# One core, two transformer layers: transposes between the scores, a key buffer filled by POOL, and a split normalization in layer 1's attention

## The chip, the core and the metric

The kernel runs on one core of a Trainium2 chip. A core has five engines that run their own instruction streams in order and wait for each other through semaphores: PE (TensorE, matrix multiplication), DVE (VectorE), ACT (ScalarE), POOL (GpSimd) and SP (SyncE), which here only issues DMA transfers. The metric is the device time of one execution in microseconds (us); lower is better. "Weight load" (PEld) is PE's loading of the stationary operand.

## The reference

The input `x` is [8, 512, 256] in float32. Two pre-norm layers follow each other, each `x = x + attention(layernorm(x))`, then `x = x + ffn(layernorm(x))`:

- layer 0: causal attention, 16 heads of 16; then a gated FFN whose inputs and weights are quantized to FP4 in blocks of 16;
- layer 1: attention with biases in which a query sees only the 64 keys up to itself; then a gated FFN with integer weights.

The part that the change touches is layer 1's attention:

```python
q = (x @ Wq + bq).reshape(B, S, H, hd).transpose(0, 2, 1, 3)   # k, v likewise
scores = jnp.einsum('bhqd,bhkd->bhqk', q, k) * scale
allowed = (j <= i) & (i - j < WINDOW)                           # WINDOW = 64
attn = jax.nn.softmax(jnp.where(allowed, scores, NEG_INF), axis=-1)
out = jnp.einsum('bhqk,bhkd->bhqd', attn, v)
return out.transpose(0, 2, 1, 3).reshape(B, S, D) @ Wo + bo
```

## The kernel before

**Stages.** The whole `x` stays in SBUF, a tile `x{b}` for each of the 8 batch elements ("batches" below). The four parts of the reference run one after another; from the spans of their instructions in the trace they take about 0 to 540 us (attention 0), 540 to 797 us (FFN 0), 797 to 1120 us (attention 1) and 1120 to 1287 us (FFN 1). One function, `attention`, writes both attentions; `banded` is true for layer 1.

**Units and quads.** A unit is (batch, m): 8 of the 16 heads of a batch. A quad is half of a unit, four heads; `quads[i]` with i = 4 c + r is the r-th quad of batch c. `body` first does some opening work and then loops over i. Quad i's pass does, in this order: the scores of quad i+2 in query order (`scores`, tiles `s`), from which DVE takes the row maxima (tiles `mx`, L540); the scores of quad i in key order (`Outputs.band`, tiles `t`), with the maxima multiplied in as twelve extra rows; ACT's exponential of them (tiles `ex`, L655); POOL's selects that zero what the mask forbids (L128); and for the quads before it the products with the values (`banded_sums`, tiles `po`), the copy `oT`, and the normalized output.

**Where q and k come from.** For a unit, `pieces` projects the transposed, normalized input: matmuls into `pq` or `pk` (through `project`, L303), ACT's biased copy into bfloat16 (`qp`/`kp` part 0, L420), and DVE's remainder (`qr`/`kr`, L421). `store` then makes two more bfloat16 parts of the remainder: ACT copies part 1 (L431), POOL subtracts to get part 2 (L434), and SP sends the three parts to HBM (L437). `land` fetches them back in six slots per head, `qq` by four transfers and `kk` by three (L447), in a layout in which one 96-row product gives the six products of parts that matter. There are three `qq`/`kk` buffers; two are made by `QK` (`qq_both`, `kk_both`), the third (`qq2`, `kk2`) belongs to the attention's own pool and is made when `body` starts. Rows 96 and up of every `kk` are constants ("ones", L353) that meet the maxima.

For batches 1 to 7 of layer 1 both the weights and the input are split in a high and a low float32r half; `project` then does three pairs of halves, two matmuls (one for each 128 of the 256 inputs) a pair. The high half of the transposed input is `yT1` (ACT, L191), its low half lies in `room` (DVE, L192).

**The order of instructions** comes from a planner: it orders each engine's instructions by its own estimate of when they are ready, save those marked by `pin` (`keep_in_program_order`), which stay in the order in which they were written. PE's matmuls of the attention are pinned, ACT's copy of part 1 (L431) is pinned, ACT's normalization (`normalize`, L168) and exponentials are not. PSUM tiles come from two rings: three two-bank tiles (`s`, `t`) and two one-bank tiles (`pm`, `pt_c`, `pq`, `pk`, `pv`, `po` and others take turns), so a matmul into a new tile waits for the readers of the one two tiles back.

**Opening of layer 1's body.** FFN 0's last projections end, the third key buffer gets its ones (DVE), POOL clears the padded value buffers, `norm(1)` normalizes batch 1 on ACT (`by`), then come the scores of quad 1, the maxima of quad 0 as rows (`pm`, L567, with an ACT copy L574 and a DVE copy L575), the two transposes of batch 1 (`turned`: `pt_c`, L185, whose readers are ACT L191 and DVE L192), and the projections, stores and fetches of unit (1, 0). The biases' rows (`bo_rows`, `bo_halves`, `two_rows`) are made meanwhile by POOL memsets and ACT copies (L1109 to L1121).

**Normalization of later batches.** In quad 1 of batch c, batch c+2 is normalized: four ACT instructions, two in each half of the pass.

Of the kernel before, what the change touches and what calls it, by code (L numbers as in the profile page):

```python
# [19 lines left out]
P = 128  # L20
B, S, D = 8, 512, 256
# [25 lines left out]
def tile_two_layers(  # L47
# [246 lines left out]
        nc.scalar.copy(full, src)  # L294
        nc.gpsimd.tensor_tensor(lo, full, hi.bitcast(F32), ALU.subtract)

    def project(dst, lhs, rhs):

        n = 0
        pairs = PAIRS if len(lhs) == 2 else ((0, 0),)  # L300
        for l, r in pairs:
            for e in range(NE):
                pin(nc.tensor.matmul(  # L303
                    dst, lhsT=lhs[l][:, e, :], rhs=rhs[r][:, e, :],
                    start=(n == 0), stop=(n == NE * len(pairs) - 1),
                ))
                n += 1
# [38 lines left out]

        return t.bitcast(BF16).rearrange("p t a (h two) -> p t a h two", two=2)[:, :, :, :, 1]

    def units_tiles(pool, n, what):
        q = pool.tile([P, 8, S], BF16, tag=f"qq{n}", name=f"qq{n}_{what}", bufs=1)  # L350
        k = pool.tile([P, 8, S], BF16, tag=f"kk{n}", name=f"kk{n}_{what}", bufs=1)

        nc.vector.tensor_copy(  # L353
            k[KF:].bitcast(F32), own[KF:].unsqueeze(2).to_broadcast([32, 8, S // 2])
        )
        return q, k
# [3 lines left out]
    def attention(home, banded, stats, norm, spin, wq_s, wk_s, wv_s, qcol, kcol, bv_bc, post, filler):  # L360
# [40 lines left out]
        def pieces(b, m, w, col, name):  # L401

            pp = psum1(f"p{name}_{b}_{m}")
            ws = halved("qk".index(name), b, w)
            project(pp, [x[:, :, m * P : (m + 1) * P] for x in ws], xT[b])
            if home[2]:
                t = home[0].tile(
                    [P, 3, S], BF16, tag=f"{name}p", name=f"{name}p_{b}_{m}", bufs=home[2]
                )
            else:  # L410
                t = home[3](f"{name}p_{b}_{m}")
            r = home[0].tile(
                [P, S], F32, tag="rem" if home[2] else "full", name=f"{name}r_{b}_{m}",
                bufs=home[2] or 1,
            )
            if col is None:
                nc.scalar.copy(t[:, 0], pp)
                nc.vector.tensor_tensor(r, pp, t[:, 0], ALU.subtract)  # L418
            else:
                nc.scalar.activation(t[:, 0], pp, AF.Identity, bias=col[:, m : m + 1])  # L420
                nc.vector.scalar_tensor_tensor(  # L421
                    r, pp, col[:, m : m + 1], t[:, 0], ALU.add, ALU.subtract
                )
            return t, r
# [44 lines left out]
        def turned(b, c):  # L469
            if c == 0:  # L470
                fine = banded and b
                xT[b] = [home[0].tile(
                    [P, NE, S], F32R if fine else F32, tag="yT1", name=f"yT{int(banded)}_{b}",
                    bufs=home[1],
                )]
                if fine:
                    xT[b].append(FINE["x"])
            spin(b, c, xT[b])
# [72 lines left out]
        def maxima(i):  # L551


            mx = MX[i]
            for a in range(2):
                nc.vector.tensor_tensor(
                    mx[:, :, a + 1, :], mx[:, :, a, :], upper(mx)[:, :, a, :], ALU.subtract
                )
# [184 lines left out]

        def body():

            q, k = units_tiles(home[0], 2, int(banded))
            QQ.append(q)
            KK.append(k)
            padded_values(home[0], 1, nc.gpsimd)
            if banded:  # L750
                for n in range(2):
                    v = home[0].tile([P, NT, H, HP], F32, tag=f"vq{n}", name=f"vq{n}", bufs=1)
                    nc.gpsimd.memset(v[WIN:, 0], 0.0)
                    VQ.append(v)
                shifted(0)
                fine = fine_halves(home[0])
                next(fine)
            norm(1)
            for i in range(1 if banded else 0, 2):
                for s in scores(i):  # L760
                    s()
                maxima(i)
            max_rows(0)
            for c in range(NE):
                turned(1, c)
            load_q(units[2])
            stores(units[2], 0)
            load_k(units[2])
            stores(units[2], 1)
            land(units[2])  # L770


            last = trail = None
            ending = filler(home[0]) if banded else None
            for i in range(len(quads) + (2 if banded else 1)):
                ts, ss, cur = [], [], None
                if i < len(quads):
                    cur = Outputs(i)
                    ts = cur.tiles()
                    if i + 2 < len(quads):  # L780
                        ss = scores(i + 2)
                c, r = i // 4, i % 4
                nT = 2 if banded else 6
                side = {p: [] for p in range(nT)}

                def at(p, fn):
                    side[p].append(fn)

                p1, p2, p3 = (1, 0, 0) if banded else (1, 2, 3)
                f1, f2, f3 = (0, 1, 1) if banded else (0, nT - 2, nT - 1)  # L790
                if banded and i + 1 < len(quads):
                    at(p3, lambda: max_rows(i + 1))

                if last is not None:
                    at(p1, lambda: last.banded_sums() if banded else last.sums((2, 3)))
                    at(p1, lambda: last.copy())
                done = trail if banded else last
                if done is not None and not banded:
                    at(p2, lambda: done.finish())

                if r == 0 and c + 1 < B:
                    at(f2 if banded else f1, lambda: values(c + 1, 0))
                if r == (2 if banded else 0) and c + 1 < B:
                    at(f1 if banded else f2, lambda: values(c + 1, 2))
                if r == 2 and c + 2 < B:
                    at(f3 if banded else f1, lambda: turned(c + 2, 0))
                    at(f3, lambda: turned(c + 2, 1))
                if r == 0 and c + 2 < B:
                    at(f3, lambda: stats(c + 2))
                if r == 1 and c + 2 < B and not banded:  # L810
                    for t in range(NT):
                        at(t, lambda t=t: norm(c + 2, [t]))
                if banded and r == 3 and c + 1 < B:
                    at(f1, lambda: shifted(c + 1))
                if r % 2 and i // 2 + 3 < len(units):
                    at(f1, lambda: load_q(units[i // 2 + 3]))
                    at(f2, lambda: load_k(units[i // 2 + 3]))
                    at(f3, lambda: stores(units[i // 2 + 3], 0))
                for p, fn in tail.pop(i, ()) if banded else ():
                    at(p, fn)  # L820
                if done is not None and banded:
                    at(p2, lambda: done.finish())
                if i + 1 < len(quads) and not banded:
                    at(p3, lambda: max_rows(i + 1))
                if cur and not banded:
                    at(f3, lambda: cur.sums((0, 1)))
                if r == 1 and c + 2 < B and banded:
                    for t in range(NT):
                        at(t // 2, lambda t=t: norm(c + 2, [t]))
                if r % 2 == 0 and i and i // 2 + 2 < len(units):  # L830
                    at(f1 if banded else p1, lambda: stores(units[i // 2 + 2], 1))
                    at(f1 if banded else f2, lambda: land(units[i // 2 + 2]))
                for p in range(max(len(ts), nT if last or done else 0)):
                    if p < len(ss):
                        ss[p]()
                        step()
                    if p < len(ts):
                        ts[p]()
                        step()
                    for fn in side[p]:  # L840
                        fn()
                    if banded and p:
                        next(fine, None)
                    if banded and i > 4 * B - 6:
                        next(ending, None)
                if ss:
                    maxima(i + 2)
                last, trail = cur, last
            for _ in ending or ():
                pass  # L850
            for n in sorted(tail) if banded else ():
                for p, fn in tail.pop(n):
                    fn()
# [615 lines left out]
```

## Time and profile before

| what | value |
|---|---|
| time, median of 3 runs | 1280.49 us (1279.89 to 1282.59) |
| the profiled execution's own time | 1288.33 us, span 1286.5 us from first to last instruction |
| mean granted PE clock | 0.954 of full speed |
| attention 1, 797 to 1120 us: busy PE, DVE, POOL, ACT | 277.4, 229.6, 211.4, 172.2 of 323 us |
| the same stretch: mean granted PE clock, DMA share | 0.95, 0.61 |

The profiled execution took 7.8 us longer than the median of the runs. A row of the page's groups, or of an answer on waits, gives a sum over instructions with one source line; a row of the timeline gives start, duration, engine, line, operation, tiles, and in brackets how long the engine stood idle before and what ended that. Idle time of an engine that isn't the bottleneck costs nothing. The label of a wait is inferred, and can name the wrong tile where several were waited for. A line "SPq" is the time at SP's queue of issuing a transfer, its own wait included.

### The profile page before, as it was taken

What the parts mean: (1) busy time and instruction counts of PE and PEld (TensorE: products, weight loads), DVE (VectorE), ACT (ScalarE), POOL (GpSimd) and SP (SyncE); (2) the same over time, 40 slices, a digit from 0 to 9 for tenths busy, and PEclk for the clock granted to TensorE, in tenths of its full rate; (3) what the DMA queues carried; (4) which work ended last, traced back from release to release, by engine and by line L of the source; (5) the groups of instructions that cost most, each with busy time, mean ns of one, the idle gap of its engine ahead of it and who ended that gap; (6) DMA issues with size and microseconds to landing.
All of it is one profiled execution on the core that took longest, in us unless ns stands there. A gap on an engine that the chain in (4) does not pass through costs nothing. (4 is left out here: it accounts for less than half of the span.)

```text
span 1286.5 us, 27214 instructions
## 1 busy us (share of the span) xinstructions
PE 1100.3 (86%) x10910; PEld 819.8 (64%) x10910; DVE 943.5 (73%) x1603; ACT 659.7 (51%) x1008; POOL 698.8 (54%) x821
## 2 busy tenths in 40 slices
PE   4778989788998888788888887788998898889998
PEld 2444444444554445787888777567777776668887
DVE  4699896698788885789799857677776686545553
ACT  3255656465674676444444333455555554455553
POOL 5165564465445566655555533576766675534443
PEclk9899999898998999899999988899999998999999
DMA  8644334443453311000000025476675676000001
GB/s 229 140 96 87 86 74 86 79 94 67 91 116 74 81 18 50 1 1 1 1 1 1 1 72 105 100 165 155 144 149 125 141 164 163 2 1 33 33 26 43
DMA packets 51634, 99.53 MB, mean 77 GB/s; under 512 B 6702, under 2 KB 43568, under 8 KB 44848
## 3 DMA queue, kind: packets, MB, share of 16 engines
q1 hardware_dynamic: 50624, 96.96, 33.9%
q8 instruction: 88, 1.44, 0.5%
q10 hardware_dynamic: 816, 0.79, 0.2%
q14 instruction: 42, 0.34, 0.1%
q0 software_dynamic: 64, 0.00, 0.0%
HBM read 61.02 MB, written 29.36 MB: 70 GB/s over the span
## 5 line engine op out<-in xcount | busy, mean ns | idle before, releaser
L128 POOL TENSOR_SCALAR_AFFINE_SELECT ex<-ex 64x512 f32<-64x512 f32 (+2 forms) x448 | 268.9, 603 | 226.1 <-ACT ex L620 131.3
L620 ACT ACTIVATE ex<-t 128x1024 f32<-128x1024 f32 (+1 forms) x192 | 167.9, 882 | 125.3 <-PE t L609 114.1
L517 DVE TENSOR_REDUCE mx<-s 128x2 f32<-128x1024 f32 (+2 forms) x192 | 196.7, 1036 | 41.1 <-PE s L506 40.3
L1319 POOL TENSOR_TENSOR hT<-gh,hT 128x512 fp32r<-128x512 f32 x48 | 61.6, 1290 | 89.6 <-ACT hT L1318 66.1
L655 ACT ACTIVATE ex<-t 128x1024 f32<-128x1024 f32 x64 | 65.5, 1023 | 86.6 <-PE t L647 81.9
L501 PE MATMUL s<-kk_both,qq_both 96*128 96x512 bf16 (+3 forms) x352 | 84.6, 323 | 20.8 <-DVE mx L517 10.9
L506 PE MATMUL s<-cmask,minus_b 128*128 128x128 bf16 (+2 forms) x352 | 90.4, 257 | 0.0
L540 DVE TENSOR_REDUCE mx<-s 128x8 f32<-128x1024 f32 x64 | 77.6, 1215 | 15.3 <-PE s L535 15.2
L282 POOL TENSOR_TENSOR h<-h,sc_h 128x704 f32<-128x704 f32 x32 | 45.1, 1410 | 79.4 <-DVE h L281 73.6
L674 PE MATMUL po<-ex,vp 128*32 128x512 f32 (+3 forms) x1024 | 83.4, 442 | 1.3 <-DVE kr L418 1.3
L609 PE MATMUL t<-qq_both,kk_both 108*128 108x512 bf16 (+3 forms) x352 | 70.9, 306 | 9.1 <-ACT ex L620 4.7
L1386 DVE SCALAR_TENSOR_TENSOR gh<-ggu,gsl 128x512 f32<-128x512 f32 x48 | 33.2, 691 | 57.1 <-ACT gsl L1384 56.6
L1260 PE MATMUL pd<-wd_high,hT 128*128 128x256 f32 x384 | 61.7, 299 | 11.6 <-DVE hT L1251 7.0
L277 ACT ACTIVATE mg_h<-h 128x704 bf16<-128x704 f32 x32 | 25.2, 788 | 82.7 <-POOL h L229 82.7
L1227 PE MATMUL gu<-wg_wgh,fyT 128*128 128x352 f32 x224 | 65.3, 333 | 2.4 <-DVE h L1234 2.4
L501 PEld LDWEIGHTS <-qq_both 96*128 96x128 bf16 x352 | 33.0, 103 | 51.6 <-issue 38.0
L229 POOL TENSOR_TENSOR h<-h,rc_h 128x704 f32<-128x704 f32 x32 | 46.4, 1449 | 34.1 <-DVE rc_h L228 18.8
L1260 PEld LDWEIGHTS pd<-wd_high,hT 128*128 128x128 f32 x384 | 53.7, 200 | 16.4 <-DVE hT L1251 10.7
L1227 PE MATMUL gu<-wu_wuh,fyT 128*128 128x352 f32 x224 | 62.7, 322 | 0.0
L1375 PE MATMUL ggu<-yT,wg_r 128*128 128x512 f32 x192 | 57.6, 412 | 2.1 <-DVE yT L1319 1.1
L279 DVE SCALAR_TENSOR_TENSOR h<-mg_h,h 128x704 f32<-128x704 bf16 x32 | 40.6, 1269 | 22.4 <-ACT mg_h L277 22.4
L674 PEld LDWEIGHTS po<-ex,vp 128*32 128x32 f32 x1024 | 27.1, 109 | 43.9 <-issue 29.8
(335 smaller groups left out, 3167.9 us busy)
## 6 DMA issues: line engine op xcount, KB each, us to landing
q_hbm<-qp SPq DMA_DIRECT2D x90, 128.0 KB
k_hbm<-kp SPq DMA_DIRECT2D x90, 128.0 KB
qq_both<-q_hbm SPq DMA_DIRECT2D x44, 256.0 KB
kk_both<-k_hbm SPq DMA_DIRECT2D x22, 384.0 KB
qq_both<-q_hbm SPq DMA_DIRECT2D x44, 128.0 KB
kk_both<-k_hbm SPq DMA_DIRECT2D x22, 256.0 KB
qq<-q_hbm SPq DMA_DIRECT2D x20, 256.0 KB
vq<-vp SPq DMA_DIRECT2D x8, 512.0 KB
```

The costliest lines, as they stand in the source:

```text
L128: nc.gpsimd.affine_select(out=t, in_=t, compare_op=ALU.is_ge, fill=0.0, base=base, pattern=[[0, n] for n in shape[1:-1]] + [[sign, shape[- ...
L501: pin(nc.tensor.matmul(bank[:, a * w : (a + 1) * w], lhsT=q[:KF, hs[j], t * P : w], rhs=k[:KF, hs[j], :w], start=(a == 0), stop=False, ski ...
L506: pin(nc.tensor.matmul(bank.rearrange("p (i k) -> p i k", k=w)[:, :, t * P :], lhsT=minus_b, rhs=cmask[:, : len(part), :], start=False, st ...
L517: nc.vector.tensor_reduce(dst, src, AX.X, ALU.max)
L540: nc.vector.tensor_reduce(mx[:, t2 : t2 + 2, :], sc.rearrange("p t (j k) -> p t j k", k=P), AX.X, ALU.max)
L609: pin(nc.tensor.matmul(bank[:, a * w : (a + 1) * w], lhsT=k[: KF + 12, self.hs[j], t * P : (t + 1) * P], rhs=q[: KF + 12, self.hs[j], t * ...
L620: nc.scalar.activation(ex[:, :banks, :used], sc[:, :banks, :used], AF.Exp, scale=QSCALE)
L655: nc.scalar.activation(ex, sc, AF.Exp, scale=QSCALE)
L674: pin(nc.tensor.matmul(self.o[HP * j : HP * (j + 1), t * P :], lhsT=vp[:, t, 4 * c + j, :], rhs=self.ex[t, j], start=(t == 0), stop=(t == ...
L1227: nc.tensor.matmul(gu[:, i, :352], lhsT=YT[b][l][:, e, t * P : (t + 1) * P], rhs=w[r][:, e, f], start=(n == 0), stop=(n == 3 * NE - 1),)
L1260: nc.tensor.matmul(pd[:, :D], lhsT=hT[l][:, k, :], rhs=wd_halves[r][:, k, :], start=(l == r == k == 0), stop=(l == 1 and k == NH - 1),)
L1319: engine.tensor_tensor(lo, src, hi.bitcast(F32), ALU.subtract)
```

## The change

Four edits, all for layer 1's attention (layer 0 keeps its code paths):

1. `project` gets a flag `last`, used by `pieces`: the three pairs of halves go high-high, low weight with high input, high weight with low input. Before, the low input was in the second pair.
2. The ones of the third key buffer are written by POOL and not by DVE.
3. In the opening, `max_rows(0)` comes first, each of the two transposes of batch 1 stands after one of the two score tiles of quad 1, and `maxima(1)` is written after unit (1, 0)'s fetches.
4. In the program, the normalization of batch c+2 moves from both halves of quad 1's pass to the second half of quad 1 and the first half of quad 2.

```diff
-    def project(dst, lhs, rhs):
+    def project(dst, lhs, rhs, last=False):
...
         for l, r in pairs:
+            if last:
+                l, r = r, l
             for e in range(NE):
...
-    def units_tiles(pool, n, what):
+    def units_tiles(pool, n, what, engine=nc.vector):
...
-        nc.vector.tensor_copy(
+        engine.tensor_copy(
             k[KF:].bitcast(F32), own[KF:].unsqueeze(2).to_broadcast([32, 8, S // 2])
         )
...
-            project(pp, [x[:, :, m * P : (m + 1) * P] for x in ws], xT[b])
+            project(pp, [x[:, :, m * P : (m + 1) * P] for x in ws], xT[b], True)
...
-            q, k = units_tiles(home[0], 2, int(banded))
+            q, k = units_tiles(home[0], 2, int(banded), nc.gpsimd if banded else nc.vector)
...
-            for i in range(1 if banded else 0, 2):
-                for s in scores(i):
+            if banded:
+                max_rows(0)
+                for c, s in enumerate(scores(1)):
                     s()
-                maxima(i)
-            max_rows(0)
-            for c in range(NE):
-                turned(1, c)
+                    turned(1, c)
+            else:
+                for i in range(2):
+                    for s in scores(i):
+                        s()
+                    maxima(i)
+                max_rows(0)
+                for c in range(NE):
+                    turned(1, c)
             load_q(units[2])
             stores(units[2], 0)
             load_k(units[2])
             stores(units[2], 1)
             land(units[2])
+            if banded:
+                maxima(1)
...
-                if r == 1 and c + 2 < B and banded:
-                    for t in range(NT):
-                        at(t // 2, lambda t=t: norm(c + 2, [t]))
+                if r in (1, 2) and c + 2 < B and banded:
+                    for t in (0, 1) if r == 1 else (2, 3):
+                        at(2 - r, lambda t=t: norm(c + 2, [t]))
```

What the planner makes of it, read from the order of the built instructions on each engine: no instruction is added or dropped but for the one copy that goes from DVE to POOL. ACT's four normalizations of each batch stand where they stood. What edit 4 does change is another instruction: for the units (2, 1), (3, 1), (4, 1), (5, 1) and (6, 1), the pinned copy of the key's part 1 (L431) now stands ahead of ACT's exponential of the first half of quad 2, where it stood behind it and behind the copy of the maxima. POOL's subtraction (L434) of these units goes ahead of the four selects of that exponential, and on SP the second and third store of the key parts go ahead of the first two fetches of `qq`. Edits 1 to 3 change nothing beyond the opening but the order of the matmuls within a projection. In the opening, DVE's order becomes: maxima of the first score tile, copy of quad 0's maxima rows, low half of transpose 0, maxima of the second score tile, low half of transpose 1. ACT copies both transposes before it touches the bias rows.

## The prediction

> **What bounds the kernel now.** I read the page first, then the busy time by stage, then who waited for whom in attention 1, then the timelines of the places concerned.
>
> ```profile
> PE 1100.3 (86%) x10910; PEld 819.8 (64%) x10910; DVE 943.5 (73%) x1603; ACT 659.7 (51%) x1008; POOL 698.8 (54%) x821
> ```
>
> PE is busy for 86% of the span, and in attention 1 for 277.4 of 323 us; the next, DVE, for 229.6. So in this stage a gap of PE that goes away is time, and work of the others counts where PE waits for it. PE's waits there, from 797 to 1100 us (total, times, longest):
>
> ```profile
> PE s L535 <- DMA kk_both<-k_hbm: 8.2, 3, 6.0
> PE pk L303 <- ACT oT L695: 4.9, 1, 4.9
> PE pq L303 <- DVE room L192: 3.7, 1, 3.7
> ...
> PE s L535 <- DMA q_hbm<-qp: 2.2, 1, 2.2
> ...
> PE s L535 <- DMA kk<-k_hbm: 1.2, 1, 1.2
> ```
>
> Two kinds matter: one wait of 3.7 us in the opening, and score matmuls (L535) that wait for fetched q and k. The opening, PE, then DVE:
>
> ```profile
> 799.62 1.40 PE L185 MATMUL pt_c<-ident,by 128*128 128x128 f32 x8
> 804.71 1.22 PE L303 MATMUL pq<-yT,qkv_wg 128*128 128x512 f32 x2 [3.68 <-DVE room L192]
> ```
>
> ```profile
> 797.97 2.51 DVE L353 COPY kk<-own 32x2048 f32<-32x2048 f32 x1
> 800.51 2.35 DVE L540 TENSOR_REDUCE mx<-s 128x8 f32<-128x1024 f32 x2
> 802.89 0.95 DVE L575 COPY qq_both<-qq_both 12x1536 bf16<-12x1536 bf16 x1
> ...
> 803.97 0.68 DVE L192 TENSOR_TENSOR room<-pt_c,yT 128x512 fp32r<-128x512 f32 x1
> ```
>
> `pq` needs the PSUM tile of transpose 0, whose last reader is DVE's low half, which ends at 804.65 because three DVE pieces stand before it. Afterwards PE runs slow: the twelve matmuls of `pq` and `pk` take 804.71 to 809.77, 0.42 us each, against 0.24 later on (859.65 to 861.18).
>
> The waits for fetched data come at the first score tile in quad 0 of a batch, the scores of unit (c, 1):
>
> ```profile
> 886.89 0.30 PE L535 MATMUL s<-kk,qq 96*64 96x64 bf16 x6 [2.17 <-DMA q_hbm<-qp]
> ...
> 925.25 0.36 PE L535 MATMUL s<-kk_both,qq_both 96*64 96x64 bf16 x7 [1.17 <-DMA kk_both<-k_hbm]
> ...
> 963.38 0.30 PE L535 MATMUL s<-kk_both,qq_both 96*64 96x64 bf16 x6 [0.71 <-issue]
> ...
> 1004.80 0.36 PE L535 MATMUL s<-kk,qq 96*64 96x64 bf16 x7 [1.21 <-DMA kk<-k_hbm]
> ```
>
> These are the units (2,1) to (5,1); (6,1) at 1046.12 has no gap, and (7,1) waits 6.05 us at 1083.35. ACT and SP before the second of them:
>
> ```profile
> 909.47 1.03 ACT L655 ACTIVATE ex<-t 128x1024 f32<-128x1024 f32 x1 [1.89 <-PE t L647]
> 910.52 0.58 ACT L574 CAST qq<-pm 12x512 bf16<-12x512 f32 x1
> 911.12 0.62 ACT L431 CAST kp<-kr 128x512 bf16<-128x512 f32 x1
> ```
>
> ```profile
> 914.61 0.58 SPq L437 DMA_DIRECT2D k_hbm<-kp  x1
> 915.25 0.91 SPq L447 DMA_DIRECT2D qq_both<-q_hbm  x2
> 917.59 1.23 SPq L447 DMA_DIRECT2D kk_both<-k_hbm  x3
> ```
>
> The key's remainder `kr` is ready at 907.85 (DVE 907.10 + 0.75), but its copy comes at 911.12, POOL's subtraction at 913.42, the last store at 914.61, the last fetch by 918.8.
>
> **What the Trainium skill says.** "TensorE: Matmul & The Clock Gate", section "What's actually happening": PE's clock halves after an idle window of about 3.4 us and comes back after as much activity. The trace agrees: 0.42 against 0.24 us above, and a granted clock of 0.50 from 888 to 890 us, after the 2.17 us gap. "DMA: Bandwidth & Descriptors", section "Issuing engines are not separate DMA queues": all transfers share 16 engines and interleave. The trace fits: the DMA share is 0.94 to 1.08 from 917 to 925 us, so an earlier fetch is worth only what room it finds. "GPSIMD Engine Reference", section "Engine selection": for one input POOL runs at about the line rate. Its 512-element casts of layer 0 (L433) take 0.609 us.
>
> **The change part by part.**
>
> *Ones by POOL, transposes between scores (edits 2 and 3).* After the change DVE's chain is: last `x` addition to 797.94; `pm` goes first on PE (797.4 to 797.8), the first score tile is done by about 798.8; maxima 798.9 to 800.1 (half of 2.35); ACT's rows (L574) still end at 800.31, since the normalizations before them end at 799.64; DVE's copy 800.4 to 801.35; low half 0 to 802.05, as transpose 0 follows the last normalization and ACT copies it by 800.95. `pq` can start at 802.1, 2.6 us earlier. The second maxima (to 803.2) and low half 1 (to 803.9) follow. PE's longest gap there shrinks to about 0.5 us, so I expect the warm 0.24 us a matmul.
>
> *Pair order (edit 1).* With the new order the first four matmuls need only high halves and end at 803.05; the last two wait for low half 1, so `pq` ends at about 804.4. In the old order four would stand behind it: 0.5 us more. From batch 2 on `room` is complete long before: no wait for it shows, so the swap costs and brings nothing there.
>
> So PE would finish `pk` at about 805.8 for 809.8. But ACT has work in between. POOL's memsets of 797.60 to 802.16 come later by the length d of the ones' copy, which no row shows on POOL: 2048 elements at the cast's rate are 4 x 0.609 = 2.4 us; from below 1.8, the memset of 2048 (L327), from above 3.9, twice the 1.94 us of a two-input operation on 1024. `two_rows` (ended 803.28) then ends at 805.7, and ACT's `qp`, next in its queue, starts there in place of 807.67. Behind it are `kp`, the two parts, and the first exponential (813.31); POOL's twelve selects, `rs_c`, the normalizations of batch 2 and PE's second big wait (4.92 us, `pk` at 826.35) hang on those. The gain that reaches them is 2.0 us for ACT's start plus 1.2 for `pk` being ready without ACT's 1.52 us wait ahead of `kp`: 3.2 us. With d at 1.8 or 3.9 it is 3.8 or 1.7; it is nothing from d of 5.6 up.
>
> *Key part moved ahead (edit 4).* In unit (3,1) the copy can go at 907.85 and ends at 908.5, in the 1.89 us in which ACT waits for `t`: that idle time hides it. POOL subtracts from 909.1 (end of the query's part) to 910.3, in its idle time before the select at 910.57. The stores are out by 910.9 and not 915.2; the four `qq` fetches by 912.8, `kk` (2.3 us after the store, as before) by 914.5 for 918.8. The values' shifts (L398, L399), next in SP's queue, move up too, and together these are 768 + 768 + 896 KB, at the 200 GB/s seen from 919 to 927 us 12.2 us, so done by 923.5 with `kk` about 1 us before; PE wants it at 924.1. The gaps then go: 2.17 + 1.17 + 0.71 + 1.21 = 5.3 us. After the first gap PE also ran slow: from 886.89 to the end of the transposes before the values took 7.68 us, in the next batch 7.88 less 1.76 of output matmuls = 6.12; that adds 1.5. I take off 0.4 for unit (6,1), where `kr` ends at 1031.24, after the exponential that started at 1029.92, and which now waits for it; and 0.9 because the margin above is only 1.6 us. Sum: 5.5 us; from below 0 (fetches no sooner), from above 6.8.
>
> Layer 0, FFN 0 and FFN 1 issue the same instructions. What follows attention 1, the 6.05 us wait of unit (7,1) included, has its order unchanged and moves as a whole.
>
> Sum against the profiled execution: 1288.3 - 3.2 - 5.5 = 1279.6. The runs have the median 1280.49; I take the same difference from it: 1271.8, rounded to 1272.
>
> **Rivals.**
>
> *The fetches come no sooner.* The DMA engines are full from 917 on, and the shifts of the values (896 KB) move up with the fetch. If `kk` still lands when all is through, only the opening gains: 1280.5 - 3.2 = 1277.3. Against it: from 905 to 911 the DMA share is 0.04 to 0.35, so there is room before.
>
> *The opening gains nothing.* POOL takes over 5 us for the ones; ACT's `qp` comes as late as before. Then 1280.5 - 5.5 = 1275. Against it: the cast's rate.
>
> *Slower: ACT's exponential behind the key part.* ACT is in order, and the copy now waits for `kr` ahead of the exponential. It decides as soon as `kr` ends later than 0.62 us before `t` is ready. In (6,1) it does, and the exponential slips by 1031.24 + 0.62 - 1029.92 = 1.9 us; POOL's selects and the next maxima rows queue behind it. If the earlier flow makes that the rule in five units and PE feels all of it, 9.7 - 3.2 = 6.5 us are lost: 1287. Against it: in the other four the margin is 0.3, 1.0, 1.0 and 1.9 us, and PE's three two-bank tiles let it run on.
>
> *No change.* The waits that go are replaced by others of equal length (maxima, `pt_c`): 1280.
>
> That the normalization itself runs later, as the edit reads, I don't expect: ACT's order holds it in place.
>
> **Numbers.** Both parts 0.60 (1268 to 1276 by itself); no sooner fetches 0.15; opening nothing 0.10; slower 0.08; no change 0.07. A measurement tells about 0.2%, 2.6 us: the first and third cases are faster, of the second two thirds. Faster 0.81, same 0.11, slower 0.08. The range runs from 1268 (both at their upper ends, 3.8 + 6.8 = 10.6, and some more warm time) to 1279.
>
> **What would show it.** Right: `pq` starts about 2.5 us after transpose 0 instead of 4 to 5; the matmuls of `pq` at 0.24 us; ACT's first exponential 3 us earlier after the end of FFN 0; the score tiles of (2,1) to (5,1) without a DMA gap; the last `k_hbm` store of these units before the `qq` fetches. Wrong: the ones' copy over 4 us on POOL; gaps at L535 of the same length; exponentials of quad 2 that wait for L431.

## The result, and the profile after

The changed kernel takes 1289.38 us (median of 18 runs, 1283.44 to 1297.55); the kernel before, timed beside it, 1283.55 us (18 runs, 1277.20 to 1290.30). The ratio is 1.0052, 95% interval 1.0034 to 1.0070: the change costs 6 to 7 us. The forecast was 1272 us, faster; it has the wrong sign. The profiled execution took 1292.1 us, with a span of 1290.1 us.

The page has hardly moved in the shares, PE 85% for 86%. A line further down, which stands word for word in the page of before too and which the prediction doesn't use, turns out to matter: a DMA queue of the kind "instruction", with 88 transfers and 1.44 MB.

```profile
PE 1100.0 (85%) x10910; PEld 821.4 (64%) x10910; DVE 939.5 (73%) x1602; ACT 659.5 (51%) x1008; POOL 699.1 (54%) x822
...
q8 instruction: 88, 1.44, 0.5%
```

PE's waits from 797 to 1100 us (who waited for whom: total, times, longest):

```profile
PE s L538 <- DMA kk_both<-k_hbm: 7.1, 2, 6.1
PE pk L306 <- ACT oT L698: 4.9, 1, 4.9
PE po L689 <- issue: 4.6, 2, 2.7
...
PE s L538 <- DMA kk<-k_hbm: 2.9, 2, 1.7
...
PE t L650 <- issue: 2.4, 1, 2.4
PE s L538 <- DMA q_hbm<-qp: 2.1, 1, 2.1
```

The wait for `room` in the opening is gone from the top. But score matmuls still wait for fetched data, and "issue" rows have grown: PE stood still although nothing that the profile follows held it up. (All of PE's "issue" rows from 835 to 1075 us sum to 8.5 us, for 6.8 before.)

**The opening came out better than forecast.** The timelines of PE, DVE, POOL and ACT there:

```profile
801.50 0.79 PE L306 MATMUL pq<-yT,qkv_wg 128*128 128x512 f32 x2 [0.39 <-DVE room L192]
```

```profile
798.34 1.22 DVE L543 TENSOR_REDUCE mx<-s 128x8 f32<-128x1024 f32 x1 [0.90 <-PE s L538]
799.78 0.95 DVE L578 COPY qq_both<-qq_both 12x1536 bf16<-12x1536 bf16 x1 [0.21 <-ACT qq_both L577]
800.76 0.69 DVE L192 TENSOR_TENSOR room<-pt_c,yT 128x512 fp32r<-128x512 f32 x1
```

```profile
797.11 1.89 POOL L356 COPY kk<-own 32x2048 f32<-32x2048 f32 x1 [1.08 <-PE pd L1271]
799.05 1.81 POOL L330 MEMSET vp<- 128x2048 f32 x1
800.92 0.52 POOL L756 MEMSET vq<- 64x512 f32 x1
```

```profile
803.38 0.30 ACT L1132 CAST two_rows<-bo_rows 128x128 fp32r<-128x128 f32 x1 [0.28 <-POOL bo_rows L1129]
803.77 0.69 ACT L423 ACTIVATE qp<-pq,qcol 128x512 bf16<-128x512 f32 x1
...
808.60 1.03 ACT L658 ACTIVATE ex<-t 128x1024 f32<-128x1024 f32 x1
```

`pq` starts at 801.50 for 804.71 and the first exponential at 808.60 for 813.31 (0.5 us of each because FFN 0 ended earlier in this execution). At the transposes of batch 2 the changed kernel is 5.0 us ahead (834.91 for 839.90). That lead and 3.3 us more are lost by FFN 1's first transposes (1130.76 for 1127.46).

**The four score tiles** that the forecast had freed of their gaps, units (2,1) to (5,1), in PE's timeline:

```profile
881.20 0.30 PE L538 MATMUL s<-kk,qq 96*64 96x64 bf16 x6 [1.71 <-DMA kk<-k_hbm]
...
923.85 0.30 PE L538 MATMUL s<-kk_both,qq_both 96*64 96x64 bf16 x6 [2.12 <-DMA q_hbm<-qp]
...
962.66 0.30 PE L538 MATMUL s<-kk_both,qq_both 96*64 96x64 bf16 x6
...
1001.24 0.30 PE L538 MATMUL s<-kk,qq 96*64 96x64 bf16 x6 [1.14 <-DMA kk<-k_hbm]
```

One of the four gaps is gone, (4,1); three stay, 1.71 + 2.12 + 1.14 = 4.97 us for 5.26 before. Of these the 2.12 us of unit (3,1), which the profile puts to a store of q, turn out below to be something else; for fetched data PE waits only 1.71 + 1.14 = 2.85 us here. And there are new stops in places where no data can be missing:

```profile
1001.97 0.28 PE L650 MATMUL t<-qq_both,kk_both 108*64 108x128 bf16 x2
...
1004.66 0.43 PE L650 MATMUL t<-qq_both,kk_both 108*64 108x128 bf16 x4 [2.42 <-issue]
...
1043.00 0.32 PE L689 MATMUL po<-ex,vp 128*32 128x64 f32 x6
1046.04 0.22 PE L689 MATMUL po<-ex,vp 128*32 128x64 f32 x1 [2.72 <-issue]
```

PE stops in the middle of a tile, between matmuls that read the same buffers, for 2.4 and 2.7 us. After the first stop it also runs at half clock:

```profile
1002.00:1005.00 3.00, 0.58 (x17) 0.42 (x13) 1.23 (x1) 0.00 (x0) 0.28 (x1) 0.71 0.62 167
1005.00:1008.00 3.00, 3.00 (x24) 2.67 (x21) 0.79 (x1) 2.22 (x3) 1.30 (x2) 0.50 0.22 77
```

(The columns are the stretch, its length, the busy time of PE, PEld, DVE, ACT and POOL, then PE's granted clock, the DMA share and GB/s.) DMA transfers by queue, in two windows of 1 us, 1002 to 1003 and then 1042 to 1043, show what else happens at these stops:

```profile
q1 hardware_dynamic: 35, 0.15, 70.3%
q8 instruction: 1, 0.02, 8.2%
```

```profile
q1 hardware_dynamic: 42, 0.18, 111.2%
q8 instruction: 1, 0.02, 9.9%
```

A transfer of the instruction queue runs at each. The trace has its times: 16 KB from 1002.01 to 1003.33, and from 1042.91 to 1044.50. PE goes on at 1004.66 and 1046.04, that is 1.3 and 1.5 us after the end of the transfer.

The Trainium skill, "Runtime: NRT & Kernel Launch", section "Instruction fetch mechanics", says that an engine's sequencer fetches its program in blocks of 16 KiB, 256 instructions, by a DMA queue of its own while it executes the block before, and that the cost is mostly hidden. The trace agrees on the size: 88 transfers for PE's 10910 matmuls and 10910 weight loads make 248 a transfer, and 16 KB each. On "mostly hidden" it agrees in part: of the 41 blocks fetched from 802 to 1109 us most cost nothing, but six stop PE for 1.5 to 2.7 us, as the experiments below show. The theories:

- For the first four experiments, **A**: edit 4 is the part that costs, whatever the mechanism. **B**: the pair order costs in every projection. **C**: the opening's gain is given back later whatever else is changed.
- For those after them, **D**: edit 4 bunches DMA traffic, blocks of PE's instructions come late through the full DMA engines, and PE runs dry. **E**: only the order of data transfers matters, PE's instructions have no part.

### The profile page after: what moved, and what is told of

Read it like the earlier page. It is cut to its first block, busy times and chain, and to the rows that moved or that the text cites. A ratio compares the mean times of both kernels' runs of the same rounds, so it can differ in the third digit from the quotient of the medians.

```text
span 1290.1 us, 27219 instructions
## 1 busy us (share of the span) xinstructions
PE 1100.0 (85%) x10910; PEld 821.4 (64%) x10910; DVE 939.5 (73%) x1602; ACT 659.5 (51%) x1008; POOL 699.1 (54%) x822
## 3 DMA queue, kind: packets, MB, share of 16 engines
q8 instruction: 88, 1.44, 0.5%
## 5 line engine op out<-in xcount | busy, mean ns | idle before, releaser
L1271 PE MATMUL pd<-wd_high,hT 128*128 128x256 f32 x384 | 61.3, 298 | 11.5 <-DVE hT L1262 6.8
L529 PE MATMUL s<-wmask,minus_b 128*64 128x512 bf16 x256 | 55.1, 406 | 0.0
```

The costliest lines, as they stand in the source:

```text
L1271: nc.tensor.matmul(pd[:, :D], lhsT=hT[l][:, k, :], rhs=wd_halves[r][:, k, :], start=(l == r == k == 0), stop=(l == 1 and k == NH - 1),)
```

## The experiments

**Which edit costs.** Four kernels, each timed against before. Edits 1 to 3 alone are the changed kernel with the old normalization call:

```diff
-                if r in (1, 2) and c + 2 < B and banded:
-                    for t in (0, 1) if r == 1 else (2, 3):
-                        at(2 - r, lambda t=t: norm(c + 2, [t]))
+                if r == 1 and c + 2 < B and banded:
+                    for t in range(NT):
+                        at(t // 2, lambda t=t: norm(c + 2, [t]))
```

> Edits 1 to 3 alone (pair order, ones by POOL, transposes between the scores); the normalization stays where it was, and so does the key's part 1. Theory A (the key part moved ahead is what costs): the opening's 4 to 5 us, seen at 825 us in the changed kernel's trace, stay to the end: about 0.996 of before, 4 to 5 us faster. Theory B (the reversed pair order costs in every projection, and the key part is not at fault): slower than before or equal, 1.000 to 1.005. Theory C (an opening that is ahead is given back later whatever else is changed): equal, 0.999 to 1.001.

Measured: 1279.02 us, 0.9960 (0.9945 to 0.9975).

Edit 4 alone is the kernel before with the reverse of that diff.

> Edit 4 alone: the normalization split over two quads, with the key's part 1 moved ahead of the exponential in units (2,1) to (6,1). My recorded step says 5.5 us faster (0.9957). Theory A: the whole loss and the opening's gain too have to come from here: 8 to 11 us slower (1.006 to 1.009). Theories B and C: within 2 us of before (0.9985 to 1.0015).

Measured: 1292.78 us, 1.0070 (1.0050 to 1.0091).

Edit 1 alone is the kernel before with the new `project` and `last=True` where `pieces` calls it.

> Edit 1 alone: in each projection of q and k for batches 1 to 7 the matmuls with the low half of the input come last. My recorded step says about nothing from batch 2 on, and up to 0.5 us gain in the opening. Theory B: 5 to 10 us slower (1.004 to 1.008). Theories A and C: within 1.5 us of before (0.999 to 1.001).

Measured: 1283.57 us, 0.9999 (0.9983 to 1.0015).

The changed kernel without edit 1 has that argument taken away again.

> Edits 2 to 4 without the pair order. Theory A: as the changed kernel, 1.004 to 1.006. Theory B: the loss is gone, 0.996 to 0.998. Theory C: 1.003 to 1.006.

Measured: 1289.76 us, 1.0043 (1.0026 to 1.0061).

So B and C fall: the pair order does nothing, and the opening keeps 4 to 5 us to the end when edit 4 is away. Edit 4 costs 9 us alone, and 10 to 12 us on top of edits 1 to 3 (by the medians and by the ratios). It moves no normalization on ACT, as forecast; it moves one ACT copy, one POOL subtraction and two DMA issues in each of five units. In the four units (2,1) to (5,1) the exponentials are not held up by the copy. In unit (3,1) of the changed kernel, ACT's timeline:

```profile
905.15 0.62 ACT L434 CAST kp<-kr 128x512 bf16<-128x512 f32 x1 [0.31 <-DVE kr L424]
...
907.12 1.03 ACT L658 ACTIVATE ex<-t 128x1024 f32<-128x1024 f32 x1 [1.35 <-PE t L650]
```

The exponential waits for `t` long after the copy is done. Only in (6,1) does it follow the copy directly, some 1.7 us later than before, as the prediction said for that unit (1030.86 for 1029.92, though the changed kernel is 0.8 us ahead there). The two profiles, edits 1 to 3 and changed, differ by 10.3 us of span. Between the starts of the transposes of each batch (L185 on `pt_c`, as in the opening for batch 1; last the scores of unit (7,1) and FFN 1's transposes), it lies here:

| stretch | edits 1 to 3 | changed | difference |
|---|---|---|---|
| batch 3 to 4 | 40.15 | 42.24 | +2.1 |
| batch 4 to 5 | 39.12 | 41.01 | +1.9 |
| batch 5 to 6 | 38.24 | 37.33 | -0.9 |
| batch 6 to 7 | 41.62 | 45.40 | +3.8 |
| batch 7 to scores of (7,1) | 47.15 | 51.45 | +4.3 |
| to FFN 1 | 44.54 | 43.68 | -0.9 |

The two largest are the stretches with the stops at 1002 and 1043 us, 2.4 and 2.7 us and the slow clock after them. Batch 4 to 5 holds the 2.12 us at 923.85. In that execution a block's transfer runs from 920.87 to 922.24, so this gap looks like a late block too; in edit 4 alone the profile puts the same gap to "issue".

```profile
924.41 0.30 PE L535 MATMUL s<-kk_both,qq_both 96*64 96x64 bf16 x6 [1.35 <-issue]
```

In the kernel with edits 1 to 3, the block that belongs to the stop at 1002 is fetched from 995.78 on, in a window from 995 to 997 us that is as full as the others; PE reaches that place 2.6 us later and runs through it without a long stop.

```profile
q1 hardware_dynamic: 78, 0.38, 102.1%
q8 instruction: 1, 0.02, 4.7%
```

```profile
998.34 0.64 PE L650 MATMUL t<-qq_both,kk_both 108*64 108x128 bf16 x7
```

Counted in PE's own stream, that transfer starts with 5,832 of PE's instructions still to come in the kernel with edits 1 to 3, and with 5,776 to come in the changed one: 56 instructions later. For the block of the stop at 1043 it is 4,667 and 4,518: 149 later. In the changed kernel PE has only 1 and 23 instructions left before the places where it stops.

**Is it PE's instruction stream?** If blocks come late, moving their borders moves the stops, though no work moves. Small matmuls that nobody reads go into a stretch around 30 us in which PE idles 8.5 us in layer 0 (64 of them take 2.03 us there):

```diff
+            if not banded:
+                pad = psum1("pad")
+                for _ in range(64):
+                    pin(nc.tensor.matmul(
+                        pad[:, 0:64], lhsT=minus_b, rhs=minus_b[:, 0:64], start=True, stop=True
+                    ))
             if banded:
                 for s in scores(0):
```

In the changed kernel:

> The changed kernel with 64 small matmuls (128 PE instructions) into a PSUM tile that nobody reads, put into the 8.5 us in which PE idles at 30 us; after them everything is the same, only each PE instruction stands 128 places later in PE's stream. Theory D (edit 4 costs because blocks of PE's own instructions, about 256 each, land 2 to 5 us late in the fuller DMA engines, at four places): the stops of 2.4 us inside a score tile t near 1002 us and of 2.7 us inside po near 1044 us go from these places, other blocks may come late elsewhere; the time moves by 3 us or more, probably down, to 1280 to 1286. Theory E (the order of data transfers alone delays work; PE's instructions have no part in it): the same stops at the same instructions, 1.004 to 1.007 of before.

Measured: 1290.57 us, 1.0033 (1.0014 to 1.0051). Both stops left their places. The score tile `t` of the first runs through,

```profile
1007.03 0.36 PE L650 MATMUL t<-qq_both,kk_both 108*64 108x128 bf16 x7
```

and stops stand elsewhere, again in the middle of a tile:

```profile
943.16 0.31 PE L689 MATMUL po<-ex,vp 128*32 128x64 f32 x1 [2.35 <-issue]
966.88 0.58 PE L538 MATMUL s<-kk_both,qq_both 96*64 96x128 bf16 x7 [2.04 <-issue]
```

That is D's sign, and E, which had the same stops at the same instructions, falls. The time, though, didn't come down as I thought likely: about as many new late blocks took the place of the old ones.

The same matmuls in the kernel before:

> The kernel before with the same 64 matmuls. Theory D: other places of late blocks, so the time may move as well, within 4 us either way (0.997 to 1.003). Theory E: as before, less what a warmer PE brings after the matmuls at 38 us (0 to 2 us).

Measured: 1289.93 us, 1.0046 (1.0032 to 1.0060), outside what I had expected: 6 us lost although no work of any engine was changed but 2 us of idle PE filled.

And in edits 1 to 3:

> Edits 1 to 3 (which gave 0.996) with the same 64 matmuls. Theory D: the two late blocks seen there (3.2 and 4.2 us late near 881 and 897 us) move; time within 4 us of 1279 either way. Theory E: 1277 to 1279.

Measured: 1285.26 us, 1.0020 (0.9997 to 1.0042); 6 us lost here as well, more than the 4 us I had allowed.

The traces tie the stops to the blocks more firmly than two stops that move. Count how many of PE's instructions (weight loads, matmuls, semaphore instructions) are still to come when PE goes on after a stop, and divide by 256. In the changed kernel the rest is 143 after each of six stops: at 848.84, 900.16, 1004.66 and 1046.04 us, and also at 923.85, the gap of unit (3,1), and at 884.00, which the profile puts to ACT:

```profile
884.00 0.59 PE L570 MATMUL pm<-minus_b,mx 128*12 128x128 bf16 x4 [1.47 <-ACT ex L658]
```

With the 64 small matmuls, 128 instructions, the rest is 15 at every such stop, which is 143 + 128 less 256. So PE stops at the borders of blocks of 256 instructions. In the twenty traces together it stops 58 times for 1 us or more at such a border between 797 and 1110 us, each time until 1.2 to 1.7 us after the end of a transfer of the instruction queue; all 53 waits of that length with the label "issue" are among them. Below, "late blocks" are stops at these borders.

**Is it the order of SP's queue?** Edit 4 has two sides: the key's parts are made earlier, and SP, which issues in order, now sends all three key stores before the first fetch of `qq`. This kernel keeps ACT's, POOL's, DVE's and PE's order as changed and gives SP its order of before (`store` calls its last argument after its first DMA):

```diff
+        def stored_and_landed(u):
+            n = (2 * u[0] + u[1]) % NB
+            far = IN_HBM.pop((u, 0))
+            kfar = store(*HALF.pop((u, 1)), f"k{u[0]}_{u[1]}",
+                         lambda: fetch(QQ[n], QS, far, (0, 1)))
+            fetch(QQ[n], QS, far, (2, 3))
+            fetch(KK[n], KS, kfar, (0, 1, 2))
```

> The changed kernel with SP's order of before in units (2,1) to (6,1): two fetches of qq go ahead of the key's stores 2 and 3. ACT's and POOL's order stays as changed. If the new order of SP's queue is what costs (all twelve transfers in one bunch): most of the loss goes, 0.996 to 0.999. If the earlier key part itself is (its transfers start earlier in any order): as the changed kernel, 1.003 to 1.006.

Measured: 1282.82 us, 0.9986 (0.9967 to 1.0004). Two DMA issues in five units are worth 0.0066 against the changed kernel, 8.5 us. SP's issues for unit (4,1), first the changed kernel, then this one:

```profile
948.41 1.93 SPq L440 DMA_DIRECT2D k_hbm<-kp  x3
950.45 1.79 SPq L450 DMA_DIRECT2D qq_both<-q_hbm  x4
953.54 1.23 SPq L450 DMA_DIRECT2D kk_both<-k_hbm  x3
```

```profile
943.66 0.57 SPq L440 DMA_DIRECT2D k_hbm<-kp  x1
944.35 0.87 SPq L455 DMA_DIRECT2D qq_both<-q_hbm  x2
945.31 1.26 SPq L440 DMA_DIRECT2D k_hbm<-kp  x2
946.62 0.94 SPq L455 DMA_DIRECT2D qq_both<-q_hbm  x2
949.79 2.08 SPq L455 DMA_DIRECT2D kk_both<-k_hbm  x3
```

Against the start of the transposes of batch 5, which lie nearest (952.90 and 948.14), the first fetch of `qq` goes out 2.5 us ahead in the changed kernel and 3.8 us ahead here. The last fetch of `kk` is no sooner here, it is out 3.7 us after that start for 1.9 us. In the eight microseconds from 6 us ahead to 2 us behind that start the DMA engines move 1.17 MB in the changed kernel and 1.39 MB here (0.85 MB before the change). The 0.22 MB are 1.1 us of the engines at 200 GB/s. What is left runs as one burst: in slices of half a microsecond, the engines stay at 90% or more for 11.5, 10.5, 13.0, 12.5 and 10.5 us on end in the five units of the changed kernel, and for 8.0, 8.0, 7.5, 8.0 and 8.5 us here (9.5, 7.5, 8.5, 8.5 and 8.5 before). PE's waits from 876 to 1075 us with SP's order of before:

```profile
PE pp L1102 <- ACT oT L713: 3.7, 4, 0.9
PE t L665 <- issue: 3.6, 1, 3.6
PE pt_o L185 <- DVE vp L392: 3.0, 5, 1.0
```

No score matmul waits for a fetch: the four gaps of 5.26 us together, which the forecast wanted gone, are gone. One long stop for a late block is left, 3.59 us at 999.68.

**Is it the full DMA engines?** The largest transfer that can be left out is the shifted copy of the values. Both kernels without it from batch 2 on (their products then read old values):

```diff
-                if banded and r == 3 and c + 1 < B:
+                if banded and r == 3 and c + 1 < 2:
                     at(f1, lambda: shifted(c + 1))
```

> The changed kernel without the transfers of the shifted values of batches 2 to 7 (L401, L402: 896 KB a batch are left out, so the products of these batches read old values). Theory D: with a third of each burst gone, the blocks of PE's instructions land in time; the stops near 1002 and 1044 us and the DMA waits at L538 go; 10 to 16 us faster than the changed kernel, 0.991 to 0.997 of before. If PE's instructions come late for a reason of their own, the stops stay and it gains only the DMA waits, 3 to 5 us: 1.001 to 1.003.

Measured: 1275.86 us, 0.9929 (0.9904 to 0.9954).

> The kernel before without the same transfers, the control. Theory D: fewer late blocks to lose here; 4 to 8 us faster, 0.994 to 0.997; so the changed kernel without them is 3 to 8 us faster than this one, which is the edit's worth as forecast with the full DMA engines out of the way.

Measured: 1280.66 us, 0.9975 (0.9961 to 0.9990). (In both, the planner also puts two fetches of `qq` elsewhere in units (c,0).) So leaving them out gains 0.0123 (16 us) in the changed kernel and 0.0025 (3 us) in the one before, and with the DMA engines relieved the change is 0.0046, 5.9 us, faster than before. The gain before fell short of the 4 to 8 us expected. In the changed kernel without the shifts both stops are gone; late blocks cost 2.9 us for 12.2, and no score tile of the four waits for data. The waits that stand for the 2.9 us:

```profile
PE s L538 <- issue: 2.0, 2, 1.1
...
PE po L689 <- issue: 0.9, 1, 0.9
```

The start of the transfers says the same in all twenty traces (the first 86 of each). Where data kept the engines under 10% busy in the microsecond before, 725 transfers, none started with fewer than 135 instructions left to the border at which PE would stop; in the middle it was 266, one block and a few instructions more. Of the 63 that started with fewer than 50 left, 59 came after a microsecond with the engines at 90% or more, none after one under 60%. The transfer itself also takes longer after such a full microsecond: 1.34 us in the middle, for 1.05 after a quiet one.

**How much is placing, how much is edit 4's own?** SP's order of before with 32 and 96 of the small matmuls:

> The changed kernel with SP's order of before, and 32 small matmuls (64 PE instructions) at 30 us. It has one long stop left, 3.6 us near 999 us. Theory D: that block's border stands 64 instructions earlier in the work, so the stop changes its place or size; 0.994 to 1.000, and about 1276 us if no other block falls into a burst. Theory E: 0.9986 as without the matmuls.

Measured: 1278.78 us, 0.9974 (0.9957 to 0.9990).

> As the kernel with 64, but 96 small matmuls (192 PE instructions). Theory D: again other places of the late blocks; 0.994 to 1.002. Theory E: 0.9986.

Measured: 1277.83 us, 0.9947 (0.9925 to 0.9969), the fastest kernel here.

The changed kernel and edits 1 to 3 at these two placings:

> The changed kernel with 32 small matmuls (64 PE instructions) at 30 us. If edit 4's loss is alignment alone: within 3 us of the next kernel, either sign. If SP's order costs at any placing: 3 to 9 us slower than the next kernel; about 1.001 to 1.006 of before.

Measured: 1284.45 us, 1.0008 (0.9992 to 1.0024).

> Edits 1 to 3 with the same 32 matmuls, the control: 0.995 to 1.002.

Measured: 1283.04 us, 0.9986 (0.9966 to 1.0006).

> The changed kernel with 96 small matmuls (192 PE instructions). As for 32: within 3 us of the next kernel if alignment alone, 3 to 9 us slower if SP's order costs at any placing. With SP's order of before the same placing gave 0.9947.

Measured: 1287.58 us, 1.0021 (1.0004 to 1.0037).

> Edits 1 to 3 with the same 96 matmuls, the control: 0.995 to 1.002.

Measured: 1280.72 us, 0.9987 (0.9970 to 1.0005).

And the kernel before:

> The kernel before with 32 small matmuls (64 PE instructions) at 30 us. Edits 1 to 3 gave 0.9986 at this placing; if their gain is the opening's 3 to 5 us at any placing, this one is at 1.001 to 1.003. If placing decides it, anything from 0.996 to 1.005.

Measured: 1288.45 us, 1.0045 (1.0028 to 1.0063).

> The kernel before with 96 small matmuls (192 PE instructions). Edits 1 to 3 gave 0.9987 here: 1.001 to 1.003 if the opening's gain holds at any placing; 0.996 to 1.005 if placing decides it.

Measured: 1286.34 us, 1.0022 (1.0004 to 1.0039).

All together, as ratios to the kernel before without small matmuls (each with an interval of about 0.002 to either side):

| PE's stream moved by | before | edits 1 to 3 | changed | changed, SP's order of before |
|---|---|---|---|---|
| 0 | 1 | 0.9960 | 1.0052 | 0.9986 |
| 64 instructions | 1.0045 | 0.9986 | 1.0008 | 0.9974 |
| 128 | 1.0046 | 1.0020 | 1.0033 | not run |
| 192 | 1.0022 | 0.9987 | 1.0021 | 0.9947 |

Three things follow. At equal placing edits 1 to 3 gain 0.0040, 0.0059, 0.0026 and 0.0035, 3.3 to 7.6 us: a gain each time, though the third by no more than the intervals leave open, so their worth doesn't hang on one lucky placing. Edit 4 costs 0.0092, 0.0022, 0.0013 and 0.0034: positive each time, though only the first and the last by more than the intervals leave open; the first is 0.006 to 0.008 larger than the others, and that part goes with the placing. And the whole change, 0.52% slower at the shipped placing, is 0.37% and 0.13% faster and equal at the others; the kernel before happens to stand at its best placing of the four. SP's order of before gains 0.0066, 0.0034 and 0.0074 over the changed kernel wherever it was run.

In the profiles, the stops for late blocks from 797 to 1110 us and, after the stroke, the waits for data at the four score tiles sum to (us):

| PE's stream moved by | before | edits 1 to 3 | changed | changed, SP's order of before |
|---|---|---|---|---|
| 0 | 6.0 / 5.3 | 4.5 / 4.3 | 12.2 / 2.9 | 3.8 / 0 |
| 64 instructions | 2.1 / 4.6 | 3.5 / 5.1 | 9.0 / 1.1 | 7.8 / 0.8 |
| 128 | 7.2 / 2.3 | 7.8 / 3.4 | 10.9 / 1.4 | not run |
| 192 | 6.6 / 2.7 | 4.1 / 2.4 | 13.7 / 2.0 | 4.2 / 0 |

Each is one execution, and executions of one kernel differ by up to 18 us in time, so single entries mean little. But at all four placings edit 4 has it both ways: less waiting for data, as forecast, and more for late blocks, by 3.1 to 9.6 us. SP's order of before keeps the first and undoes the second, wholly or in part.

## Why the prediction was wrong

**The opening (forecast 3.2 us) was right in mechanism and sized too small.** Edits 1 to 3 gain 0.0040, 5.1 us. `pq` started 2.7 us sooner once the earlier end of FFN 0 is taken off (3.21 - 0.50), for the 2.6 forecast, and ran warm. The mis-sized term is ACT's start of `qp`: it was said to gain 2.0 us, as POOL's ones would hold up `two_rows` by 2.4 us. It gained 3.4 us (807.67 to 803.77, less 0.5). The copy took 1.89 us for 2.4, and the first memset of `vq` behind it took 0.52 us where it had taken 1.49 before, so `two_rows` came only 0.9 us later than before (803.68 for 803.28, and 0.5 for the earlier end of FFN 0).

**The pair order at nothing was right:** 0.9999 alone.

**The key part moved ahead (forecast 5.5 us gained) is where it failed.** The issue times were forecast well up to the stores. In unit (3,1), with the 2.35 us added by which the changed kernel is ahead at the nearest transposes, those of batch 4 (911.89 for 914.24), the copy ends at 908.1 for the forecast 908.5, POOL subtracts until 909.6 for 910.3, and the stores are out by 911.1 for 910.9. The `qq` fetches follow by 914.2 for 912.8 and `kk` by 915.6 for 914.5. The step that failed is the one from there to the gain: "together these are 768 + 768 + 896 KB, at the 200 GB/s seen from 919 to 927 us 12.2 us ... The gaps then go", and with it the sum of 5.5 us, in which the new order of SP's queue and the supply of PE's instructions stand at nothing. The recorded change names the order (the stores ahead of the first two `qq` fetches), and the sum gives no price for it.

This is what the runs show in its place. Those two fetches had been ready without the key, and had filled the DMA engines while the key's parts were made. Behind the stores they wait for POOL's subtraction, and the exchange of about 2.4 MB then runs as one block of 10.5 to 13.0 us, about the length that was forecast. The gaps for data did shrink, from 5.26 to 2.85 us in the two profiles. But PE needs a new block of its own instructions every 7.6 us on average (the 41 from 802.74 to 1108.52), and in such a burst they come late: these stops went from 6.0 to 12.2 us, and edit 4 cost 9 to 12 us instead of gaining 5.5. With SP's order of before, and everything else of edit 4 as forecast, the four gaps went: the sum 2.17 + 1.17 + 0.71 + 1.21 was sound, the order that should have brought it wasn't.

**Late blocks were there before.** The rows with "issue" in the profile of before, 1.84 us at 854.13 and 2.03 us at 982.36 among them, are the same kind of stop: a block's transfer ran from 979.75 to 981.08, and PE went on at 982.36. The forecast counted full DMA engines only against the fetch of `q` and `k`. (The row of 0.71 us at 963.38, with the same label, lies at no border; counting it among the waits for data was right.)

**The rivals.** "The fetches come no sooner" named the right place, the full engines, and at two of the four tiles a wait for data stayed; but it priced edit 4 at zero, and its 1277.3 us missed the stops of PE. The slower rival, exponentials held up by the copy, had the right sign by the wrong mechanism: in the four units with margin ACT waited for `t` after the copy, not the other way. "The opening gains nothing" fell with the copy's 1.89 us.

**The clock.** The prediction said that the trace agrees with an idle window of about 3.4 us. The stretches at half clock do last that long or twice that (887.79 to 891.20, 802.46 to 809.28), but the first of them followed a gap of 2.17 us, and the half clock of the changed kernel at 1003.24 set in inside a stop of 2.4 us: here less unbroken idle time than that window was enough.

**Size of the base.** The three runs shown for before had the median 1280.49 us; over 18 to 75 runs it is 1282.65 to 1284.02. The forecast stood on a base some 3 us low, which explains nothing of its sign.

**Open.** The trace shows when a block's transfer starts, not when it was asked for. That late starts go with full engines is shown; whether the request waits in a queue behind data packets is not. The Trainium skill, "DMA: Bandwidth & Descriptors", section "Queues, rings and completion order", says that each DMA engine goes round the queues packet by packet; the transfers of blocks, 0.9 us at their shortest and up to 2.2 us here, fit sharing with data packets, but don't prove it. How far edit 4's cost in the many runs divides as it does in single profiles isn't settled. Nor is where the kernel before loses its 2.8 to 5.9 us with the small matmuls: attention 1 takes 330.3 us in its profile without them, and 326.5, 327.3 and 330.6 with them. Comparisons at equal placing have the same matmuls on both sides.

## What to carry to other kernels

When an edit moves a store ahead in an in-order DMA queue, price what it now stands in front of: a fetch that was ready waits with it, and a burst that was spread becomes one block. On an engine with a long unrolled program, its own instructions are a client of the same DMA engines: look for stops in the middle of a tile, for the instruction queue's transfers beside them, and for stops that lie a multiple of 256 instructions apart, whatever their label. And a difference of half a per cent between two such kernels can come from a few small matmuls that move the stream, so repeat the comparison with the stream moved by some dozens of instructions before you believe that an edit is good or bad.

## What the runs showed of the hardware that was not expected

- Blocks of PE's instructions come late through full DMA engines. In 58 stops of 1 us or more PE resumed 1.2 to 1.7 us after the end of its block's transfer and 2.4 to 3.4 us after its start (1004.66 after 1002.01 to 1003.33, for one), so a block whose transfer starts less than about that ahead of need stops PE. The stop of 2.4 us was followed by half clock from 1005 to 1010.
- The blocks are fetched one ahead: the transfer after which PE resumes is the one that had just ended, and with idle engines it starts about 266 instructions ahead of need, one block of 256 and a few more.
- Small matmuls that nobody reads, which move PE's stream by 64 to 192 instructions, made the kernel before 0.22% to 0.46% slower, 2.8 to 5.9 us.
- POOL's copy of 32 x 2048 float32 took 1.89 us, less than DVE's 2.51 us for the same copy.
